# Expert sums, convolution taps and two products of a Mamba and mixture-of-experts block move from VectorE to ScalarE and GpSimd

## The chip, the cores and the metric

The kernel runs on one core of one Trainium2 chip. The core has a TensorE for matrix products, a VectorE, a ScalarE, a GpSimd and a SyncE, which here only issues DMAs. The metric is the device time of one execution in microseconds (us). Each engine works through its own instructions in order; it stands when the next one waits for another engine.

## The reference

Input: x of 4 x 1024 rows of 128 features, fp32. Three parts follow each other, each with a layernorm in front and added to x:

```
x = x + 0.5 * ffn(layernorm(x))
x = x + mamba(layernorm(x))
x = x + 0.5 * ffn(layernorm(x))

ffn(x):                                  # 8 experts, all of them for every row
  cw = softmax(x @ w_router) * softmax((x @ w_gating) / 0.1);  cw = cw / (sum(cw) + 1e-9)
  out = sum over e of cw[:, e] * ((silu(x @ w_gate[e]) * (x @ w_up[e])) @ w_down[e])   # 128 -> 512 -> 128

mamba(x):                                # 256 inner features, 16 states, 4 taps
  xs, z = split(x @ W_in)
  xc = silu(causal_conv4(xs) + conv_b)
  dbl, B, C = split(xc @ W_x);  dt = softplus(dbl @ W_dt + b_dt)
  h[t] = exp(dt * A) * h[t-1] + (dt * xc) * B;   y[t] = sum over states of h[t] * C
  out = ((y + xc * D) * silu(z)) @ W_out
```

## The kernel before

**Tiling.** The 4096 rows are eight blocks of 512 (a batch has two). Tiles have features or hidden units in the 128 partitions and the 512 rows of a block along the free axis. There are 16 feed-forward passes (two per block) and eight Mamba passes. The list `order` gives the sequence of the feed-forward passes: the first part of blocks 0 to 3, then second and first parts by turns, at last second parts alone.

**Clock of the program.** A group is one expert of one pass: four chunks of 128 hidden units. In a group, TensorE first makes gate and up products of four chunks (`gu`, L435 to L437: three matmuls each, since the operands are split into a high and a low fp32r part), then the down products of four chunks of the expert before (`down`, L478, fp32, two instructions each), which add up in the PSUM tile `pd`. There is one `pd` buffer; `pg` and `pu` have two each. A group has eight slots: slots 0 to 3 stand in front of the four `gu`, 4 to 7 in front of the four `down`. All else is hung on slots: pass s starts at slot 64 s, block k of the Mamba part at START[k], and its steps at fixed distances from there (layernorm, transposes, projection `xsproj`, convolution `conv`, `act`, `xproj`, `dtproj`, `softplus`, `dtfin`, then eight pairs of states in `exps`, then `zproj`, `gate`, `outproj`). A pass runs beside a Mamba block most of the time, and TensorE's instructions are in the order of the slots.

**One expert on the other engines.** ScalarE takes SiLU of `pg` into `h` (L438), VectorE multiplies by `pu` (L444), and the down products read `h`. After the fourth down product VectorE multiplies `pd` by the expert's weight, which a DMA has broadcast into `cwb` (L491, for the first expert L488), and GpSimd adds the result to `acc` (L493; in the first and the last pass VectorE does it). When a pass is over, `ffn_end` transposes `acc` on TensorE and adds it to x.

**One state of the Mamba part.** ScalarE makes `da`, exp(dt * A), in two halves (L643). VectorE makes `hb`, `dx` times the broadcast B row (`prod`, L651, written to PSUM), two scans over time (`step`, L656) and the product with C (`read`, L667, back into `da`). GpSimd adds `da` to `y` (L678). The addition is held back until the next `prod` has been issued and waits for its end ("shared SBUF port"). The B and C rows come in `bcb` tiles by DMA, three buffers ahead.

**The planner.** `Plan` keeps a clock per engine with fixed costs and orders VectorE's instructions while the program is written: the product L444 is placed when it should be ready (`now`), small steps go to a list `hi`, the states to a list `lo`. `need` places whatever a next step depends on at once. The order is then fixed; the chip only follows it. `misc` hands out the one PSUM bank that all small products and transposes share, and a new use waits for the last reader.

The convolution before: ScalarE makes the first tap with the bias (L581), VectorE adds the three other taps, two halves each (L587, six instructions per block). `dtfin` multiplies `dt` by `xc` on VectorE (L633), `gate` multiplies the SiLU of z by `y` on VectorE (L702). Table loads on ScalarE stand between SiLU and exponentials.

Of the kernel before, what the change touches and what calls it, by code (L numbers as in the profile page):

```python
# [21 lines left out]
BIG = 10  # L22
START = (80, 168, 272, 368, 472, 568, 672, 784)
N0 = 36
SPR = 1.56
EPI = 130
XP = 23
BU = -4
WIDE = 8
EARLY = 3  # L30
# [9 lines left out]
GT = 4  # L40
PO = 10
FN = -1
FT = 2
# [7 lines left out]
PREL = -12  # L51
FEND = 12
OUT = 3
SL = 0.35
# [73 lines left out]
def tile_macaron_mamba_moe(  # L128
# [78 lines left out]

    wrg = sb.tile([P, P], F32, tag="tmp", bufs=2, name="wrg")
    V.memset(wrg, 0.0)
# [86 lines left out]
    ffn = {}  # L296
    silu_at, h_at = {}, {}

    def ffn_events(s):
# [25 lines left out]
        def logits():  # L325
            plan.need(lambda: "xl" in d)
            xh, xl = d["xh"], d["xl"]
            lt = misc(f"lt_{nm}")
            T.matmul(lt, wrg_h, xh, start=True, stop=False)
            T.matmul(lt, wrg_h, xl, start=False, stop=False)  # L330
            T.matmul(lt, wrg_l, xh, start=False, stop=True)
            ls = d["ls"] = sb.tile([NE2, TB], F32, tag="tmp", bufs=2, name=f"ls_{nm}")
            S.copy(ls, lt[0:NE2, :])
            d["ls_at"] = plan.on_act(0.65, plan.on_pe(0.7, d["low"][4]))
# [50 lines left out]
        def cwt():  # L385
            plan.need(lambda: "cw" in d)
            pt = misc(f"cwt_{nm}")
            for j in range(J):
                T.transpose(pt[0:E, j * P : (j + 1) * P], d["cw"][:, j, :], ident)
            ct = sb.tile([E, TB], F32, tag="tmp", bufs=2, name=f"ct_{nm}")  # L390
            S.copy(ct, pt[0:E, :])
            plan.on_act(0.62, plan.on_pe(0.44, d["cw2"][4]))
            cd = d["cd"] = dr.tile([E, TB], F32, tag="cd", bufs=2, name=f"cd_{nm}")
            nc.sync.dma_start(out=cd, in_=ct)
            for e in range(2):
                load_cw(s, e)
# [18 lines left out]
    def gu(s, c):  # L415
# [29 lines left out]

        h_at[g] = d["h_at", c] = plan.now(mul, 0.6, t, SL)
        if q == 1:
# [13 lines left out]
    def down(s, c):  # L461
        d = ffn[s]
        kind, k = order[s]
        e, f = divmod(c, FC)
        if f == 0:
            plan.need(lambda: not d.get("tmp") or d["tmp"][3])
            d["pd"] = ps.tile([P, TB], F32, tag="pd", bufs=1, name=f"pd_{kind}_{k}_{e}")
            if e + 2 < E:
                load_cw(s, e + 2)
        h = d.pop(("h", c))  # L470
        if len(h) == 2:
            w = d["wds", e][:, :, f * H : (f + 1) * H]
            T.matmul(d["pd"], w[:, 0, :], h[0], start=(f == 0), stop=False)  # L473
            T.matmul(d["pd"], w[:, 0, :], h[1], start=False, stop=False)  # L474
            T.matmul(d["pd"], w[:, 1, :], h[0], start=False, stop=(f == FC - 1))  # L475
            t = plan.on_pe(0.69, d["h_at", c])
        else:
            T.matmul(d["pd"], wd[e][:, f * H : (f + 1) * H], h[0], start=(f == 0), stop=(f == FC - 1))  # L478
            t = plan.on_pe(0.86, d["h_at", c])
        if f < FC - 1:  # L480
            return
        cwb = d.pop(("cwb", e))
        pd = d["pd"]

        def weigh():
            if e == 0:
                d["acc"] = sb.tile([P, TB], F32, tag="acc", bufs=2, name=f"acc_{kind}_{k}")
                V.tensor_tensor(d["acc"], pd, cwb, ALU.mult)  # L488
            else:
                tmp = sb.tile([P, TB], F32, tag="tmp", bufs=2, name=f"tmp_{kind}_{k}_{e}")  # L490
                V.tensor_tensor(tmp, pd, cwb, ALU.mult)  # L491
                eng = V if s in (0, len(order) - 1) else G
                eng.tensor_tensor(d["acc"], d["acc"], tmp, ALU.add)  # L493
                d["acc_at"] = plan.on_pool(1.3, plan.dve)

        d["tmp"] = plan.put(weigh, 0.6, t)

    def ffn_end(s):
        kind, k = order[s]
        d = ffn.pop(s)  # L500
        plan.need(lambda: d["tmp"][3])
        pt = misc(f"fo_{kind}_{k}")
        for j in range(J):
# [10 lines left out]

        plan.reader = plan.put(upd, 0.6, plan.on_pe(0.44, d["acc_at"]))

    carry = {}
    busy = set()
    for k in range(NBLK):
        for q in range(NS // 2):  # L520
            busy.add(START[k] + (WIDE if k else 0) + N0 + 8 * int(SPR * q))

# [11 lines left out]

    riders = []

    def mamba_events(k):
# [38 lines left out]
        def conv(i):  # L576
# [8 lines left out]

            def tap(q):
                V.scalar_tensor_tensor(  # L587
                    cv[:, i, :], xs[:, i, q : q + TB], cw_sb[:, i, q : q + 1], cv[:, i, :],
                    ALU.mult, ALU.add,
                )  # L590
                if q < 3:
                    plan.put(lambda: tap(q + 1), 0.67)
                else:
                    d["conv"] = d.get("conv", 0) + 1
                    d["cv_at"] = plan.dve + 0.1

            plan.put(lambda: tap(1), 0.67, plan.on_act(0.9))

        def act():
            plan.need(lambda: d.get("conv") == ND)  # L600
            xc = d["xc"] = sb.tile([P, ND, TB], F32, tag="xc", bufs=1, name=f"xc_{nm}")
            S.activation(xc, d["cv"], AF.Silu)
            d["xc_at"] = plan.on_act(1.05, d["cv_at"], "silu")

# [26 lines left out]
        def dtfin():  # L631
            dx = d["dx"] = big(f"dx_{nm}")
            plan.put(lambda: V.tensor_tensor(dx, d["dt"], d["xc"], ALU.mult), 1.14, d["spt"])  # L633
            y = d["y"] = sb.tile([P, ND, TB], F32, tag="y", bufs=2, name=f"y_{nm}")
            for i in range(ND):
                S.activation(y[:, i, :], d["xc"][:, i, :], AF.Copy, scale=D_sb[:, i : i + 1])
            plan.on_act(1.22)

        def exps(n):
# [4 lines left out]
            t = plan.on_act(1.22, 0.0, "exp")  # L644
            for f, cost in ((prod, 1.14), (lambda n: step(n, 0), 1.16), (lambda n: step(n, 1), 1.16), (read, 1.14)):
                plan.put(lambda f=f: f(n), cost, t, low=True)

        def prod(n):
            bcb = d["bcb", n]
            hb = d["hb"] = ps.tile([P, ND, TB], F32, tag="hb", bufs=1, name=f"hb_{nm}_{n}")  # L650
            mul = V.tensor_tensor(hb, d["dx"], bcb[:, 0:1, :].to_broadcast([P, ND, TB]), ALU.mult)  # L651
            flush(mul)

# [7 lines left out]
        def read(n):  # L661
# [7 lines left out]
            pump()  # L669
            d["add"] = da  # L670
            if n == NS - 1:
                flush(None)
                d["scanned"] = d["y_at"]

        def flush(after):
            da = d.pop("add", None)
            if da is not None:
                ins = G.tensor_tensor(d["y"], d["y"], da, ALU.add)  # L678
                d["y_at"] = plan.on_pool(2.4, plan.dve)
                if after is not None:  # L680
                    tc.add_manual_dep(
                        ins.ins, after.ins.name, mybir.DependencyInfo(mybir.DependencyClass.Sync, mybir.DependencyReason.DATA),
                        reason="shared SBUF port",
                    )

# [10 lines left out]
        def gate():  # L696
# [3 lines left out]

            def mul():
                V.tensor_tensor(d["yg"], d["yg"], d["y"], ALU.mult)  # L702
                d["gated"] = plan.dve + 0.1

            plan.put(mul, 1.14, d["scanned"])

        def outproj():
            plan.need(lambda: "gated" in d)
            po = misc(f"po_{nm}")
# [11 lines left out]

            plan.reader = plan.put(upd, 0.6, plan.on_pe(1.8, d["gated"]))

        w = WIDE if k else 0

        def free_slot(t):
# [7 lines left out]
            (-1 - 2 * e, ln), (NA - e, nrm), (TA, tr), (XS, inproj), (XS, lambda: xsproj(0)), (XS + 2, lambda: xsproj(1)),  # L734
            (XS + CV, lambda: conv(0)), (XS + CV + 2, lambda: conv(1)), (AP + w, act), (XP + w, xproj),
            (XP + w + 2, lambda: dtproj(0)), (XP + w + 4, lambda: dtproj(1)), (free_slot(28 + w), softplus), (DF + w, dtfin),
        ]
        for q in range(NS // 2):
            t = N0 + 8 * int(SPR * q) + w
# [8 lines left out]
        ev += [  # L748
            (EPI + v, lambda: zproj(0)), (EPI + v + 2, lambda: zproj(1)), (EPI + v + GT, gate), (EPI + v + PO, outproj),
        ]  # L750
# [4 lines left out]
    def add(base, evs):  # L755
        for t, f in evs:
            events.setdefault(max(0, base + t), []).append(f)
# [3 lines left out]
    for s in range(len(order)):  # L761
        add(8 * GPS * s, ffn_events(s))
        kind, k = order[s]
        if kind == 1 and k + 1 < NBLK:
            add(8 * GPS * s, [(8, lambda k=k: load_x(k + 1))])
        add(8 * GPS * (s + 1), [(FEND, lambda s=s: ffn_end(s))])
    for k in range(NBLK):
# [15 lines left out]
    with tc.manual_schedule(engines={ET.PE, ET.Activation, ET.DVE, ET.Pool, ET.SP}):  # L783
        grp = 0
        while events or done < nst:
            for q in range(FC):
# [3 lines left out]
                if c < nst:  # L790
                    gu(c // (GPS * FC), c % (GPS * FC))
            for q in range(FC):
                for f in events.pop(8 * grp + 4 + q, []):
# [41 lines left out]
```

## Time and profile before

| | |
|---|---|
| median of three runs | 1430.25 us (1429.8 to 1431.17) |
| the profiled execution's own time | 1429.55 us |
| its span, first to last instruction | 1427.7 us |
| TensorE busy (modelled ends) | 1315.0 us, 92% |
| VectorE busy | 1252.9 us, 88% |
| ScalarE busy | 815.0 us, 57% |
| GpSimd busy | 491.2 us, 34% |
| TensorE clock granted, mean | 0.978 |

How to read the lines: `PE` is TensorE, `PEld` its weight loads, `DVE` VectorE, `ACT` ScalarE, `POOL` GpSimd, `SP` SyncE. L491 is line 491 of the kernel. A row of a group gives line, engine, operation, output <- input, shapes and count; then busy time in us and the mean of one in ns; then the idle time of the engine just in front of these instructions and what ended it. A row of the waits gives who waited for whom: us in all, times, longest. The digits over the span are busy tenths in 40 equal slices of 35.7 us. A row of a stretch gives its bounds, its length and each engine's busy time in it. Rows with three numbers and slashes give the shortest, median and longest duration in ns.

### The profile page before, as it was taken

To read this page: it belongs to the slowest core of one execution; us is meant where nothing else is said; L and a number is where in the kernel's file an instruction comes from. 1 tells how busy PE (TensorE), PEld (TensorE's weight loads), DVE (VectorE), ACT (ScalarE), POOL (GpSimd) and SP (SyncE) were. 2 spreads that over 40 slices of the span, in tenths; PEclk is the share of its full clock that TensorE was granted. 3 is DMA by queue.
4 is the path that set the end of the run, shared out by engine and by line. 5 is a ranking of instruction groups with operands and counts; after the bars stand their busy time and mean duration, and the time that the engine had idled before them with its cause. 6 is when DMAs were issued, how large, how long until landed. Compare 5 with 4: busy or idle time off the path is not lost. (4 is left out here: it accounts for less than half of the span.)

```text
span 1427.7 us, 14522 instructions
## 1 busy us (share of the span) xinstructions
PE 1315.0 (92%) x4740; PEld 857.2 (60%) x4740; DVE 1252.9 (88%) x1819; ACT 815.0 (57%) x1220; POOL 491.2 (34%) x275
## 2 busy tenths in 40 slices
PE   6999999998998998897999899999999999996897
PEld 4665666565655665564566556655666566664675
DVE  3454699998999998999999999999999989998797
ACT  4444756756666566555676576566667575651321
POOL 1201234344433343344334433353444434432100
PEclk9999999999999999999999999999999999998999
DMA  3411233332322333333332343322433224230010
GB/s 108 136 45 32 76 106 83 88 94 67 84 83 83 105 87 73 70 89 104 73 91 81 74 113 81 104 82 68 102 84 91 75 66 112 80 89 15 8 55 20
DMA packets 71356, 113.47 MB, mean 79 GB/s; under 512 B 6960, under 2 KB 19568, under 8 KB 71280
## 3 DMA queue, kind: packets, MB, share of 16 engines
q1 hardware_dynamic: 71280, 112.54, 29.3%
q8 instruction: 37, 0.61, 0.2%
q14 instruction: 39, 0.32, 0.1%
HBM read 109.64 MB, written 2.88 MB: 79 GB/s over the span
## 5 line engine op out<-in xcount | busy, mean ns | idle before, releaser
L438 ACT ACTIVATE h<-pg 128x512 f32<-128x512 f32 x512 | 302.1, 598 | 420.0 <-PE pg L437 407.7
L678 POOL TENSOR_TENSOR y_m<-y_m,da_m 128x1024 f32<-128x1024 f32 x128 | 307.5, 2402 | 453.3 <-DVE hb_m L651 371.9
L478 PE MATMUL pd<-h,wd 128*128 128x512 f32 x920 | 418.6, 595 | 0.0
L444 DVE TENSOR_TENSOR h<-h,pu 128x512 f32<-128x512 f32 x512 | 339.7, 680 | 83.9 <-PE pu L437 73.7
L478 PEld LDWEIGHTS pd<-h,wd 128*128 128x128 f32 x920 | 172.7, 190 | 174.0 <-issue 166.1
L435 PE MATMUL pg<-xh_f,wh 128*128 128x512 f32 x512 | 258.1, 504 | 18.4 <-ACT h L438 17.6
L435 PE MATMUL pu<-xh_f,wh 128*128 128x512 f32 x512 | 211.3, 413 | 37.6 <-DVE h L444 36.9
L493 POOL TENSOR_TENSOR acc<-acc,tmp 128x512 f32<-128x512 f32 x98 | 141.9, 1448 | 260.3 <-DVE tmp L491 236.4
L437 PE MATMUL pg<-xh_f,wl 128*128 128x512 f32 x512 | 205.1, 401 | 1.0 <-POOL wl L240 1.0
L436 PE MATMUL pg<-xl_f,wh 128*128 128x512 f32 x512 | 204.4, 399 | 0.0
L436 PE MATMUL pu<-xl_f,wh 128*128 128x512 f32 x512 | 204.1, 399 | 0.0
L437 PE MATMUL pu<-xh_f,wl 128*128 128x512 f32 x512 | 203.9, 398 | 0.0
L651 DVE TENSOR_TENSOR hb_m<-dx_m,bcb_m 128x1024 f32<-128x1024 f32 x128 | 165.6, 1293 | 1.3
L656 DVE TENSOR_TENSOR_SCAN hb_m<-da_m,st_sb,hb_m 128x512 f32<-128x512 f32 x128 | 164.1, 1282 | 1.6
L643 ACT ACTIVATE da_m<-dt_m,A_sb 128x512 f32<-128x512 f32 x256 | 163.7, 710 | 0.6
L656 DVE TENSOR_TENSOR_SCAN hb_m<-da_m,hb_m 128x512 f32<-128x512 f32 x128 | 156.4, 1222 | 1.7
L667 DVE TENSOR_TENSOR da_m<-hb_m,bcb_m 128x1024 f32<-128x1024 f32 x128 | 155.6, 1216 | 1.0
L435 PEld LDWEIGHTS pu<-xh_f,wh 128*128 128x128 f32 x512 | 97.8, 191 | 86.7 <-DVE h L444 67.1
L435 PEld LDWEIGHTS pg<-xh_f,wh 128*128 128x128 f32 x512 | 98.3, 192 | 78.1 <-issue 31.5
L436 PEld LDWEIGHTS pg<-xl_f,wh 128*128 128x128 f32 x512 | 98.6, 193 | 41.9 <-issue 27.1
L437 PEld LDWEIGHTS pg<-xh_f,wl 128*128 128x128 f32 x512 | 98.0, 191 | 25.0 <-POOL wl L240 1.4
L437 PEld LDWEIGHTS pu<-xh_f,wl 128*128 128x128 f32 x512 | 97.4, 190 | 22.9
(109 smaller groups left out, 1180.5 us busy)
## 6 DMA issues: line engine op xcount, KB each, us to landing
bcb_m<-bc_m SPq DMA_DIRECT2D x128, 512.0 KB, 4.9
cwb<-cd_f SPq DMA_DIRECT2D x128, 256.0 KB, 4.1
x<-in_L_attn_x_dram SPq DMA_DIRECT2D x8, 256.0 KB, 5.5
wraw<-in_L_ffn_w_gate_dram SPq DMA_DIRECT2D x8, 256.0 KB, 3.1
wraw<-in_L_ffn_w_up_dram SPq DMA_DIRECT2D x8, 256.0 KB, 5.9
wd<-in_L_ffn_w_down_dram SPq DMA_DIRECT2D x8, 256.0 KB, 5.1
out_dram<-x SPq DMA_DIRECT2D x8, 256.0 KB, 6.3
bc_m<-db_m SPq DMA_DIRECT2D x8, 64.0 KB
```

The costliest lines, as they stand in the source:

```text
L435: T.matmul(o, wh[e][:, i, cols], d["xh"], start=True, stop=False)
L436: T.matmul(o, wh[e][:, i, cols], d["xl"], start=False, stop=False)
L437: T.matmul(o, wl[e][:, i, cols], d["xh"], start=False, stop=True)
L438: S.activation(h[:, q, :], pg, AF.Silu)
L444: V.tensor_tensor(h[:, q, :], h[:, q, :], pu, ALU.mult)
L478: T.matmul(d["pd"], wd[e][:, f * H : (f + 1) * H], h[0], start=(f == 0), stop=(f == FC - 1))
L493: eng.tensor_tensor(d["acc"], d["acc"], tmp, ALU.add)
L643: S.activation(da[:, i, :], d["dt"][:, i, :], AF.Exp, scale=A_sb[:, i, n : n + 1])
L651: mul = V.tensor_tensor(hb, d["dx"], bcb[:, 0:1, :].to_broadcast([P, ND, TB]), ALU.mult)
L656: V.tensor_tensor_scan(hb[:, i, :], d["da", n][:, i, :], hb[:, i, :], 0.0 if first else st_sb[:, i, n : n + 1], ALU.mult, ALU.add,)
L667: V.tensor_tensor(da, hb, bcb[:, 1:2, :].to_broadcast([P, ND, TB]), ALU.mult)
L678: ins = G.tensor_tensor(d["y"], d["y"], da, ALU.add)
```

## The change

The diff below is cut to what the prediction speaks of.

- **Expert sums.** In the 14 passes that are neither first nor last, ScalarE copies `pd` from PSUM to SBUF (`take`): for the first expert to `acc`, else to `tmp`. GpSimd then multiplies by `cwb` and, from the second expert on, adds to `acc`. The copy is placed after the second SiLU of the next group (TAKE) or at the latest before `pd` is used again.
- **Batches on GpSimd.** `pool_put` queues a GpSimd instruction; `pool_run` issues all that are queued, when the next `prod` has been issued, and each of them waits for that `prod`. If no state is planned, or a step needs the result (`pool_need`), they are issued at once without that wait. The additions to `y` take this way too.
- **Blocks 1 to 6** (`fast` is false): the convolution's taps are made on ScalarE, one tap of both halves per call, into tiles of their own, and GpSimd adds them up (three additions of 1024 elements). Step-size product and gate are GpSimd's. Their START is 8 slots earlier and WIDE 8 slots more, so that layernorm, projection and taps come one group earlier and `act` and the states stay at their slots. The output projection comes 4 slots later (POW).
- `ffn_end` of passes 1 to 14 but one comes at slot 15 in place of 12; `tmp` has three buffers in place of two; the planner's costs change a little.

```diff
-START = (80, 168, 272, 368, 472, 568, 672, 784)
+TMP = 3
+TAKE = 2
+START = (80, 160, 264, 360, 464, 560, 664, 784)
-WIDE = 8
+WIDE = (0, 16, 16, 16, 16, 16, 16, 8)
+FAST = (0, 7)
+POW = 4
+FENDS = 15
...
     def down(s, c):
         if f == 0:
+            while takes:
+                takes.pop(0)()
...
+        def take():
+            if e == 0:
+                d["acc"] = sb.tile([P, TB], F32, tag="acc", bufs=2, name=f"acc_{kind}_{k}")
+                S.copy(d["acc"], pd)
+                at = plan.on_act(0.58, t)
+                d["sum"] = pool_put(lambda: G.tensor_tensor(d["acc"], d["acc"], cwb, ALU.mult), 1.25, at)
+            else:
+                tmp = sb.tile([P, TB], F32, tag="tmp", bufs=TMP, name=f"tmp_{kind}_{k}_{e}")
+                S.copy(tmp, pd)
+                at = plan.on_act(0.58, t)
+                pool_put(lambda: G.tensor_tensor(tmp, tmp, cwb, ALU.mult), 1.25, at)
+                d["sum"] = pool_put(lambda: G.tensor_tensor(d["acc"], d["acc"], tmp, ALU.add), 1.25, at)
+            d["tmp"][3] = True
+            if e == E - 1:
+                pool_run(None)
+
+        if edge:
+            d["tmp"] = plan.put(weigh, 0.6, t)
+        else:
+            d["tmp"] = [None, 0, 0, False]
+            takes.append(take)
...
+    def pool_put(fn, cost, ready):
+        it = [fn, cost, ready, False, None]
+        pend.append(it)
+        if not plan.lo:
+            pool_run(None)
+        return it
+
+    def pool_run(after):
+        while pend:
+            it = pend.pop(0)
+            ins = it[0]()
+            it[3], it[4] = True, plan.on_pool(it[1], max(it[2], plan.dve))
+            if after is not None:
+                tc.add_manual_dep(
+                    ins.ins, after.ins.name, ..., reason="shared SBUF port",
+                )
+
+    def pool_need(it):
+        if not it[3]:
+            pool_run(None)
+        return it[4]
...
+        def conv_taps(q):
+            xs = d["xs"]
+            a = big(f"tap{q}_{nm}")
+            for i in range(ND):
+                if q == 0:
+                    S.activation(
+                        a[:, i, :], xs[:, i, 0:TB], AF.Identity,
+                        bias=cb_sb[:, i : i + 1], scale=cw_sb[:, i, 0:1],
+                    )
                 else:
+                    S.activation(a[:, i, :], xs[:, i, q : q + TB], AF.Copy, scale=cw_sb[:, i, q : q + 1])
+                t = plan.on_act(0.61)
+            if q == 0:
+                d["cv"] = a
+            else:
+                d["cv_it"] = pool_put(lambda: G.tensor_tensor(d["cv"], d["cv"], a, ALU.add), 2.4, t)
...
-            plan.put(lambda: V.tensor_tensor(dx, d["dt"], d["xc"], ALU.mult), 1.14, d["spt"])
+            d["dx_it"] = plan.put(lambda: V.tensor_tensor(dx, d["dt"], d["xc"], ALU.mult), 1.14, d["spt"]) if fast else pool_put(lambda: G.tensor_tensor(dx, d["dt"], d["xc"], ALU.mult), 2.4, d["spt"])
...
             mul = V.tensor_tensor(hb, d["dx"], bcb[:, 0:1, :].to_broadcast([P, ND, TB]), ALU.mult)
-            flush(mul)
+            pool_run(mul)
...
+            it = pool_put(lambda: G.tensor_tensor(d["y"], d["y"], da, ALU.add), 2.4, plan.dve)
             if n == NS - 1:
-                flush(None)
-                d["scanned"] = d["y_at"]
+                d["scanned"] = it
...
+            d["gated"] = pool_put(lambda: G.tensor_tensor(d["yg"], d["yg"], d["y"], ALU.mult), 2.4, plan.dve)
...
+            ev = [(XS + CV + 2 * q, lambda q=q: conv_taps(q)) for q in range(4)] + ev
...
+                if q == TAKE - 1:
+                    while takes:
+                        takes.pop(0)()
```

More of the change, by code (lines that the diff above doesn't have):

```diff
@@ L206, in tile_macaron_mamba_moe @@
     V.memset(nhalf, -0.5)
-    wrg = sb.tile([P, P], F32, tag="tmp", bufs=2, name="wrg")
+    wrg = sb.tile([P, P], F32, tag="tmp", bufs=TMP, name="wrg")
     V.memset(wrg, 0.0)
@@ L297, in tile_macaron_mamba_moe @@
     silu_at, h_at = {}, {}
+    takes = []
     def ffn_events(s):
@@ L331, in logits @@
             T.matmul(lt, wrg_l, xh, start=False, stop=True)
-            ls = d["ls"] = sb.tile([NE2, TB], F32, tag="tmp", bufs=2, name=f"ls_{nm}")
+            ls = d["ls"] = sb.tile([NE2, TB], F32, tag="tmp", bufs=TMP, name=f"ls_{nm}")
             S.copy(ls, lt[0:NE2, :])
@@ L389, in cwt @@
                 T.transpose(pt[0:E, j * P : (j + 1) * P], d["cw"][:, j, :], ident)
-            ct = sb.tile([E, TB], F32, tag="tmp", bufs=2, name=f"ct_{nm}")
+            ct = sb.tile([E, TB], F32, tag="tmp", bufs=TMP, name=f"ct_{nm}")
             S.copy(ct, pt[0:E, :])
@@ L444, in mul @@
             V.tensor_tensor(h[:, q, :], h[:, q, :], pu, ALU.mult)
-        h_at[g] = d["h_at", c] = plan.now(mul, 0.6, t, SL)
+        h_at[g] = d["h_at", c] = plan.now(mul, 0.62, t, SL)
         if q == 1:
@@ L483, in down @@
         pd = d["pd"]
+        edge = s in (0, len(order) - 1)
         def weigh():
@@ L489, in weigh @@
             else:
-                tmp = sb.tile([P, TB], F32, tag="tmp", bufs=2, name=f"tmp_{kind}_{k}_{e}")
+                tmp = sb.tile([P, TB], F32, tag="tmp", bufs=TMP, name=f"tmp_{kind}_{k}_{e}")
                 V.tensor_tensor(tmp, pd, cwb, ALU.mult)
[L492 to L496, printed above, removed]
+                V.tensor_tensor(d["acc"], d["acc"], tmp, ALU.add)
+                plan.dve += 0.6
+        def take():
[5 more added lines that the diff above has]
+            else:
+                tmp = sb.tile([P, TB], F32, tag="tmp", bufs=TMP, name=f"tmp_{kind}_{k}_{e}")
+                S.copy(tmp, pd)
[10 more added lines that the diff above has]
+            takes.append(take)
     def ffn_end(s):
@@ L500, in ffn_end @@
         d = ffn.pop(s)
+        while takes:
+            takes.pop(0)()
         plan.need(lambda: d["tmp"][3])
+        at = pool_need(d["sum"]) if "sum" in d else d["tmp"][4]
         pt = misc(f"fo_{kind}_{k}")
@@ L513, in upd @@
                 )
-        plan.reader = plan.put(upd, 0.6, plan.on_pe(0.44, d["acc_at"]))
+        plan.reader = plan.put(upd, 0.6, plan.on_pe(0.44, at))
     carry = {}
@@ L520, in tile_macaron_mamba_moe @@
         for q in range(NS // 2):
-            busy.add(START[k] + (WIDE if k else 0) + N0 + 8 * int(SPR * q))
+            busy.add(START[k] + (WIDE[k]) + N0 + 8 * int(SPR * q))
     stored = {}
@@ L535, in tile_macaron_mamba_moe @@
     riders = []
+    pend = []
+    def pool_put(fn, cost, ready):
[11 more added lines that the diff above has]
+                tc.add_manual_dep(
+                    ins.ins, after.ins.name, mybir.DependencyInfo(mybir.DependencyClass.Sync, mybir.DependencyReason.DATA),
+                    reason="shared SBUF port",
+                )
[3 more added lines that the diff above has]
+        return it[4]
     def mamba_events(k):
@@ L584, in conv, with tap @@
             )
[L586 to L592, printed above, removed]
-                else:
-                    d["conv"] = d.get("conv", 0) + 1
-                    d["cv_at"] = plan.dve + 0.1
-            plan.put(lambda: tap(1), 0.67, plan.on_act(0.9))
-        def act():
-            plan.need(lambda: d.get("conv") == ND)
+            t = plan.on_act(0.61)
+            if True:
+                def tap(q):
+                    V.scalar_tensor_tensor(
+                        cv[:, i, :], xs[:, i, q : q + TB], cw_sb[:, i, q : q + 1], cv[:, i, :],
+                        ALU.mult, ALU.add,
+                    )
+                    if q < 3:
+                        d["tap"] = plan.put(lambda: tap(q + 1), 0.67)
+                    else:
+                        d["conv"] = d.get("conv", 0) + 1
+                        d["cv_at"] = plan.dve + 0.1
+                plan.put(lambda: tap(1), 0.67, t)
+        def conv_taps(q):
[6 more added lines that the diff above has]
+                        bias=cb_sb[:, i : i + 1], scale=cw_sb[:, i, 0:1],
+                    )
+                else:
+                    S.activation(a[:, i, :], xs[:, i, q : q + TB], AF.Copy, scale=cw_sb[:, i, q : q + 1])
+                t = plan.on_act(0.61)
+            if q == 0:
+                d["cv"] = a
+            else:
+                d["cv_it"] = pool_put(lambda: G.tensor_tensor(d["cv"], d["cv"], a, ALU.add), 2.4, t)
+        def act():
+            if fast:
+                plan.need(lambda: d.get("conv") == ND)
+                at = d["cv_at"]
+            else:
+                at = pool_need(d["cv_it"])
             xc = d["xc"] = sb.tile([P, ND, TB], F32, tag="xc", bufs=1, name=f"xc_{nm}")
             S.activation(xc, d["cv"], AF.Silu)
-            d["xc_at"] = plan.on_act(1.05, d["cv_at"], "silu")
+            d["xc_at"] = plan.on_act(1.05, at, "silu")
         def xproj():
@@ L644, in exps @@
             t = plan.on_act(1.22, 0.0, "exp")
-            for f, cost in ((prod, 1.14), (lambda n: step(n, 0), 1.16), (lambda n: step(n, 1), 1.16), (read, 1.14)):
+            if n == 0:
+                if fast:
+                    plan.need(lambda: d["dx_it"][3])
+                else:
+                    t = max(t, pool_need(d["dx_it"]))
+            for f, cost in ((prod, 1.2), (lambda n: step(n, 0), 1.2), (lambda n: step(n, 1), 1.2), (read, 1.2)):
                 plan.put(lambda f=f: f(n), cost, t, low=True)
@@ L669, in read @@
             pump()
-            d["add"] = da
+            it = pool_put(lambda: G.tensor_tensor(d["y"], d["y"], da, ALU.add), 2.4, plan.dve)
             if n == NS - 1:
-                flush(None)
-                d["scanned"] = d["y_at"]
[L675 to L684, printed above, removed]
+                d["scanned"] = it
         def zproj(i):
@@ L699, in gate, with mul @@
             plan.need(lambda: "scanned" in d)
[L701 to L705, printed above, removed]
-        def outproj():
-            plan.need(lambda: "gated" in d)
+            if fast:
+                def mul():
+                    V.tensor_tensor(d["yg"], d["yg"], d["y"], ALU.mult)
+                at = pool_need(d["scanned"])
+                d["gated"] = plan.put(mul, 1.14, at)
+                return
+            d["gated"] = pool_put(lambda: G.tensor_tensor(d["yg"], d["yg"], d["y"], ALU.mult), 2.4, plan.dve)
+        def outproj():
+            if fast:
+                plan.need(lambda: d["gated"][3])
+                at = d["gated"][4]
+            else:
+                at = pool_need(d["gated"])
             po = misc(f"po_{nm}")
@@ L720, in upd @@
                 mixed.add(k)
-            plan.reader = plan.put(upd, 0.6, plan.on_pe(1.8, d["gated"]))
-        w = WIDE if k else 0
+            plan.reader = plan.put(upd, 0.6, plan.on_pe(1.8, at))
+        w = WIDE[k]
+        fast = k in FAST
         def free_slot(t):
@@ L734, in mamba_events @@
             (-1 - 2 * e, ln), (NA - e, nrm), (TA, tr), (XS, inproj), (XS, lambda: xsproj(0)), (XS + 2, lambda: xsproj(1)),
-            (XS + CV, lambda: conv(0)), (XS + CV + 2, lambda: conv(1)), (AP + w, act), (XP + w, xproj),
+            (AP + w, act), (XP + w, xproj),
             (XP + w + 2, lambda: dtproj(0)), (XP + w + 4, lambda: dtproj(1)), (free_slot(28 + w), softplus), (DF + w, dtfin),
         ]
+        if fast:
+            ev = [(XS + CV, lambda: conv(0)), (XS + CV + 2, lambda: conv(1))] + ev
+        else:
+            ev = [(XS + CV + 2 * q, lambda q=q: conv_taps(q)) for q in range(4)] + ev
         for q in range(NS // 2):
@@ L748, in mamba_events @@
         ev += [
-            (EPI + v, lambda: zproj(0)), (EPI + v + 2, lambda: zproj(1)), (EPI + v + GT, gate), (EPI + v + PO, outproj),
+            (EPI + v, lambda: zproj(0)), (EPI + v + 2, lambda: zproj(1)), (EPI + v + GT, gate), (EPI + v + PO + (0 if fast else POW), outproj),
         ]
@@ L765, in tile_macaron_mamba_moe @@
             add(8 * GPS * s, [(8, lambda k=k: load_x(k + 1))])
-        add(8 * GPS * (s + 1), [(FEND, lambda s=s: ffn_end(s))])
+        add(8 * GPS * (s + 1), [(FENDS if 0 < s < len(order) - 1 and order[s] != (1, NBLK - 1) else FEND, lambda s=s: ffn_end(s))])
     for k in range(NBLK):
@@ L791, in tile_macaron_mamba_moe @@
                     gu(c // (GPS * FC), c % (GPS * FC))
+                if q == TAKE - 1:
+                    while takes:
+                        takes.pop(0)()
             for q in range(FC):
```

## The prediction

> **What bounds the kernel now.** I read the engine shares first, then the slices of the span:
>
> ```profile
> PE 1315.0 (92%) x4740; PEld 857.2 (60%) x4740; DVE 1252.9 (88%) x1819; ACT 815.0 (57%) x1220; POOL 491.2 (34%) x275
> ...
> PE   6999999998998998897999899999999999996897
> ...
> DVE  3454699998999998999999999999999989998797
> ```
>
> TensorE looks busiest, but its busy time is modelled, so I check it against the time between its starts. VectorE is at 9 tenths from the sixth slice (180 us) on. Second, the timeline:
>
> ```profile
> 600.17 0.39 PE L435 MATMUL pu<-xh_f,wh 128*128 128x512 f32 x1
> 600.40 0.40 PE L436 MATMUL pu<-xl_f,wh 128*128 128x512 f32 x1
> ...
> 603.67 3.60 PE L478 MATMUL pd<-h,wd 128*128 128x512 f32 x8
> 607.10 1.95 PE L712 MATMUL po_m<-w_out_sb,zs_m 128*128 128x128 f32 x16
> ```
>
> Gate and up matmuls start 0.23 us apart; eight down matmuls take 3.43 us (603.67 to the next at 607.10), so 0.43 each. A group (four chunks, one expert) is 24 x 0.2335 + 8 x 0.428 = 9.03 us of TensorE. Third, two stretches:
>
> ```profile
> core 0: us, PE busy (x) PEld busy (x) DVE busy (x) ACT busy (x) POOL busy (x), PEclk, DMA share, GB/s
> 223.10:941.20 718.10, 661.57 (x2344) 420.57 (x2342) 675.47 (x947) 455.13 (x671) 287.48 (x156) 0.98 0.32 86
> 70.70:97.70 27.00, 27.00 (x97) 18.00 (x96) 13.97 (x26) 10.95 (x17) 2.36 (x1) 1.00 0.16 42
> ```
>
> The second row is three groups without the Mamba part: 27.0 us, 9.0 a group, VectorE half idle, so 9.03 is TensorE's own pace. The first row runs from slot 168 to slot 672, five Mamba periods, 63 groups (252 SiLUs at L438). TensorE needs there 63 x 9.03 = 569; five blocks' projections and transposes, 16 x 0.43 + 16 x 0.12 + 0.5 = 9.3 each, 46; and 7.9 passes' transposes and logits at 2.6 (three at 0.23, sixteen small ones at about 0.11), 20. Together **635 us of 718**: 83 us are lost. VectorE is busy 675 of 718. It is the bound; the waits agree:
>
> ```profile
> PE pu L435 <- DVE h L444: 36.9, 48, 2.6
> ACT xn_f L284 <- DVE nb_f L276: 15.5, 2, 8.7
> POOL y_m L678 <- DVE hb_m L651: 371.9, 92, 9.5
> ```
>
> TensorE waits for the product of SiLU and up; ScalarE stands 8.7 us at once for a layernorm's result, with SiLUs queued behind it; GpSimd mostly waits for VectorE.
>
> **The parts and their prices.** Rows:
>
> ```profile
> L491 DVE TENSOR_TENSOR tmp<-pd,cwb 128x512 f32<-128x512 f32 x112 | 76.2, 681 | 36.9 <-PE pd L478 27.4 <-PE pd L475 4.0 <-issue 3.1
> L587 DVE SCALAR_TENSOR_TENSOR cv_m<-xs_m,cw_sb,cv_m 128x512 f32<-128x512 f32 x48 | 39.4, 838 | 0.3
> L633 DVE TENSOR_TENSOR dx_m<-dt_m,xc_m 128x1024 f32<-128x1024 f32 x8 | 12.5, 1563 | 0.0
> L702 DVE TENSOR_TENSOR zs_m<-zs_m,y_m 128x1024 f32<-128x1024 f32 x8 | 10.8, 1350 | 0.4 <-POOL y_m L678 0.4
> L570 ACT COPY xs_m<-xs_m 128x512 f32<-128x512 f32 x16 | 9.4, 588 | 16.5 <-PE xs_m L569 16.5
> L636 ACT ACTIVATE y_m<-xc_m,D_sb 128x512 f32<-128x512 f32 x16 | 10.6, 713 | 0.0
> L678 POOL TENSOR_TENSOR y_m<-y_m,da_m 128x1024 f32<-128x1024 f32 x128 | 307.5, 2402 | 453.3 <-DVE hb_m L651 371.9 <-ACT da_m L643 26.9 <-DVE da_m L667 20.5
> ```
>
> *Off VectorE:* weighings of 14 of the 16 passes, 112 x 0.68 = 76; taps of six blocks, 36 x 0.838 = 30; step-size products 6 x 1.56 = 9; gates 6 x 1.35 = 8. Sum **124 us**. *Onto ScalarE:* 112 PSUM copies at the row of L570, 66; 36 tap activations at the row of L636 (SBUF to SBUF, scale per partition), 26. Sum 92, to about 907. Copy and Identity bring no table load in this trace (none stands at L570 or L581). *Onto GpSimd:* 112 products at 1.29 (the shortest common time of L493's additions), 144; 18 convolution sums, 6 step-size products and 6 gates at 2.40, 72. Sum 216, to about 708 of some 1380.
>
> In the five-period window VectorE loses 63 x 0.68 = 43 and 5 x (5.03 + 1.56 + 1.35) = 40: 675 becomes 593, below TensorE's 635. **The bound passes to TensorE, and the window cannot go below 635.** So what counts is which of the 83 lost us remain, and what is new. I walked TensorE's starts through this window. Before the first `pu` matmul, 27 us (VectorE late); before the first `pg`, 15 (ScalarE, which mostly stood for a layernorm); before the Mamba and router matmuls, 23 (VectorE holds the one `misc` bank or an operand); some 18 are scattered, part of it half-clock after long stalls. After:
> - `pu`: a product may come 1.4 us late before TensorE stands, one scan is 1.28; with VectorE near 88% I keep 8.
> - Mamba and router matmuls: 10; scattered: 7.
> - Layernorms: VectorE is early, but the power at L272 runs on GpSimd, which is now over half busy, and it stands in line behind a batch of 4 to 5 us. Between nothing and 13 x 2.5 us; I keep 8.
> - Taps on ScalarE: four pairs at slots 17, 19, 21, 23 of a block, within one group, 5.8 us beside 2.4 of SiLUs and the copy's 0.6. For blocks 2, 4 and 6 the same group also holds a pair of exponentials with two table loads (2.84 + 2.57), and a layernorm (1.9) or the router's copies. Some 15 us in a group of 9 to 11, less 1.5 of slack: 3 to 5 us. Two such blocks and something for the rest: 10. Without the stretch of down matmuls to hide in, all taps' 26 us would show.
> - The transposes at the end of a pass and the output projection wait for GpSimd chains, given 3 to 4 slots more: 8 x 0.6 = 5.
>
> That is 48, so 683 in place of 718: **35 us** gained. Outside the window: groups 84 to 115 lose 22 us now, of which I take half, 11; block 7's last wait at the output projection (9.6 us) gets 3 shorter; block 0's scans 2; the start and the last pass keep VectorE's path. Together 51: 1429.55 of the profiled execution becomes 1378.5, and against the median, 0.7 higher, **1379**.
>
> DMAs: none is added. The broadcast of the weights for expert e+2 waits for the buffer of e-1, now freed by a GpSimd product instead of VectorE's; it is issued from SP's queue ahead of `bcb` loads, which run three states (some 24 us) ahead of a landing of 4.9. I take nothing; a GpSimd 10 us late would still be covered, at 20 each scan pays the excess.
>
> **Where a rule speaks against it.** First the rows:
>
> ```profile
> L651 DVE TENSOR_TENSOR hb_m<-dx_m,bcb_m x128: 1220/1226/3294, 163.8 to 1290.9; 128x1024 f32<-128x1024 f32 x128
> L493 POOL TENSOR_TENSOR acc<-acc,tmp x98: 1264/1294/2197, 119.0 to 1355.8; 128x512 f32<-128x512 f32 x98
> ```
>
> The product at L651 (two SBUF inputs) takes 1.23 in the median and 3.29 at worst: 2.06 more, nearly one GpSimd addition. The Trainium skill ("SBUF — State Buffer", Who interferes with whom) says why: such an instruction and a GpSimd one that reads SBUF exclude each other, and the later stands until the other is done. The diff ties every batch to the end of such a product. A batch is one `y` addition and 0.8 of a weighing, 2.4 + 0.8 x 2.6 = 4.5 us; the next product comes after two scans and a reading, 3.7 at least, with `h` products between 5 to 7. By the row I take 0.3 us for a third of 80 products, 8 us, inside VectorE's 42 to spare. By the rule, with a whole addition lost each time, 80 x 2.4 = 192, and the kernel would be far slower. The row is nearer, since batches start right behind the product.
>
> Second, the skill ("GPSIMD Engine Reference", 4.1 Engine selection) sends elementwise work to VectorE, GpSimd being about twice as slow with two inputs. The rows agree on the ratio (2.38 against 1.23), and by the rule 216 us replace 124. Here that is no loss as long as GpSimd waits (372 us) for VectorE; it is one if TensorE comes to wait for it.
>
> **Rivals.**
> - *ScalarE becomes the engine that TensorE waits for.* For: in-order, some 76% busy after (455 + 37 + 22 of 680), SiLUs behind copies, taps and table loads. Against: it waits 408 us for `pg` today. If each of 56 pairs of exponentials passes on the copy's 0.6, that is 34: 1413.
> - *TensorE's floor is nearly reached:* half of the 48 stay away in the window and half as much outside: about 1343. Against: single `misc` and `pd` banks.
> - *Slower: the lock at L651.* VectorE is back at today's work when each of the 80 products of the window loses 83 / 80 = 1.04 us. If three batches in four run into the next product (taps make a batch of 12 us) and cost 1.8 each, 1.35 a product, it is 0.31 x 80 = 25 over five periods, some 35 in all: 1465. It decides from 1.04 us a product.
> - *Nothing:* the relief is real in the trace, and TensorE's floor is known; only an exact cancellation gives it.
>
> **Numbers.** Forecast case (1345 to 1395) 0.57; ScalarE's or other waits eat more (1395 to 1427) 0.22; floor 0.08; the lock, slower, 0.11; no change 0.02. Within 0.2%, about what a measurement of this kernel can tell, is 1427.4 to 1433.1. The range 1342 to 1424 leaves out the lock, no change, and 0.06 at the two ends. Faster 0.87.
>
> **What would show it.** Right: VectorE near 1130 us and below 9 tenths in many slices; waits of `pu` for VectorE down to a third; `pd` never waits for a copy; TensorE needing 9.0 to 9.5 in groups without a block's front. Wrong: L651's mean well above 1.5 us, `pg` waiting for ScalarE by 40 us or more, transposes of `acc` or `po` standing for GpSimd.

## The result, and the profile after

The changed kernel takes **1474.18 us** (median; 1470.75 to 1476.31), the kernel before 1430.03 beside it: a ratio of 1.0318, 95% interval 1.0278 to 1.0357. It is 44 us slower where 51 us less were forecast. The span of the profiled execution is 1474.5 us (1476.31 in its own time), the mean granted clock 0.965 (0.978 before).

The first part of the page and its slices, of the changed kernel:

```profile
PE 1332.7 (90%) x4740; PEld 868.5 (59%) x4740; DVE 1196.5 (81%) x1659; ACT 888.0 (60%) x1368; POOL 706.8 (48%) x417
...
PE   6998999997999998998999798979888999996797
...
DVE  4454699888877996899699979985888969997797
```

The work moved as planned: GpSimd is at 706.8 us (708 forecast), ScalarE at 888 (907). VectorE has the 160 instructions less that were planned, but its busy time fell only by 56 us, to 1196.5, where 124 were taken off it. Of the 68 that are missing, some 42 are longer instructions: summed one by one, VectorE's durations fell by 82 us. Most of these 42 is time in which an instruction stood on the shared port: the time above the usual duration of the same form went from 34 to 64 us (the median of each form, instructions over 15% above it), and each of the 65 instructions counted there ends behind the end of a GpSimd instruction, later by no more than its own usual duration and 0.15 us. The other 25 us are no new work: in the profile VectorE's instructions overlap by 75 us in place of 100, and busy time counts an overlap once. And although VectorE is below 9 tenths in many slices now, TensorE is not better served.

Stretches of the changed kernel: the five Mamba periods (groups 21 to 84) and groups 84 to 114 behind them, with the columns of the table shown before:

```profile
228.70:957.20 728.50, 668.68 (x2344) 426.12 (x2342) 629.62 (x849) 501.93 (x764) 428.86 (x244) 0.97 0.31 85
957.20:1302.40 345.20, 314.31 (x1102) 200.80 (x1101) 288.74 (x376) 216.56 (x332) 178.56 (x107) 0.96 0.29 80
```

The same groups took 718.1 and 319.3 us before: 10 and 26 us of the loss, with about 5 each in front and at the end. VectorE is at 86% and 84% there. More than half of the loss is thus behind the window that the prediction worked through, in groups for which it took a gain of 11: `pu` waits for VectorE there for 18.1 us in 10 waits, up to 4.9 each, where it was 7.4 in 12, up to 1.7. The waits of the changed kernel:

```profile
PE pu L441 <- DVE h L450: 58.4, 43, 4.9
PE fo L535 <- POOL acc L515: 19.3, 5, 7.2
PE pg L441 <- ACT h L444: 12.0, 7, 4.9
POOL y_m L754 <- DVE hb_m L735: 110.9, 40, 12.6
```

TensorE waits longer for the SiLU products than before (58.4 us against 36.9), although VectorE has a fifth of its time free; it waits for GpSimd at the ends of passes (`fo`), where it never did; and less for ScalarE's SiLU. The rows of the product that the batches are tied to, and of two router instructions:

```profile
L735 DVE TENSOR_TENSOR hb_m<-dx_m,bcb_m x128: 1220/1232/3416, 167.8 to 1314.3; 128x1024 f32<-128x1024 f32 x128
...
L380 DVE TENSOR_TENSOR cw_f<-ex_f x16: 191/193/2294, 24.8 to 1389.4; 128x32 f32<-128x32 f32 x16
...
L384 DVE TENSOR_SCALAR cs_f<-cs_f x16: 169/170/2072, 25.2 to 1390.9; 128x4 f32<-128x4 f32 x16
```

The product's mean rose from 1.293 to 1.404 us, 14 us in all. The router's instructions work on 4 to 64 numbers per partition and usually last 0.2 us, but up to 2.3 us when they stand on the port. The timeline shows how a batch does it (start, duration, engine, line; rows in between are left out):

```profile
352.66 1.23 DVE L735 TENSOR_TENSOR hb_m<-dx_m,bcb_m 128x1024 f32<-128x1024 f32 x1
354.02 1.27 POOL L514 TENSOR_TENSOR tmp<-tmp,cwb 128x512 f32<-128x512 f32 x1 [5.90 <-ACT ex_f L368]
354.28 1.10 DVE L379 TENSOR_TENSOR ex_f<-ex_f,sm_f 128x64 f32<-128x64 f32 x1
355.38 1.29 POOL L515 TENSOR_TENSOR acc<-acc,tmp 128x512 f32<-128x512 f32 x1
355.42 1.30 DVE L380 TENSOR_TENSOR cw_f<-ex_f 128x32 f32<-128x32 f32 x1
356.63 2.38 POOL L754 TENSOR_TENSOR y_m<-y_m,da_m 128x1024 f32<-128x1024 f32 x1
356.97 2.07 DVE L384 TENSOR_SCALAR cs_f<-cs_f 128x4 f32<-128x4 f32 x1
359.39 2.61 DVE L740 TENSOR_TENSOR_SCAN hb_m<-da_m,st_sb,hb_m 128x512 f32<-128x512 f32 x2
361.91 1.26 DVE L450 TENSOR_TENSOR h<-h,pu 128x512 f32<-128x512 f32 x2
362.63 0.80 PE L441 MATMUL pu<-xh_f,wh 128*128 128x512 f32 x1 [4.10 <-DVE h L450]
```

The batch starts behind the product. Three router instructions each end with one GpSimd instruction (at 355.29 and 355.38, 356.67 and 356.72, 359.01 and 359.04): 4.5 us for 0.6 us of work. The scans and the SiLU products stand behind them in VectorE's fixed order, and TensorE stands 4.1 us.

To compare the runs I use one measure besides the time: the **walk**, the time between the starts of neighbouring matmuls above their own pace (0.2335, 0.428 or 0.115 us), by what the next matmul waited for. Before, it gives 45 us for `pu` on VectorE and 19 for `pg` on ScalarE; after, 65 for `pu`, 20 for `fo` on GpSimd and 13 for `pg`. These three rows make 34 of the 47 us of span. The other large part is the half speed of the clock: gate, up and down matmuls that waited for nothing and ran in its half-speed pieces stand 33.5 us above their pace, 15.7 before. Outside these pieces the same matmuls stand 17, 19 before.

### The profile page after: what moved, and what is told of

It is laid out like the page before. It is cut to its first block, busy times and chain, and to the rows that moved or that the text cites. A ratio compares the mean times of both kernels' runs of the same rounds, so it can differ in the third digit from the quotient of the medians.

```text
span 1474.5 us, 14694 instructions
## 1 busy us (share of the span) xinstructions
PE 1332.7 (90%) x4740; PEld 868.5 (59%) x4740; DVE 1196.5 (81%) x1659; ACT 888.0 (60%) x1368; POOL 706.8 (48%) x417
## 5 line engine op out<-in xcount | busy, mean ns | idle before, releaser
L486 PE MATMUL pd<-h,wd 128*128 128x512 f32 x920 | 427.4, 603 | 0.0
L754 POOL TENSOR_TENSOR y_m<-y_m,da_m 128x1024 f32<-128x1024 f32 x128 | 311.1, 2430 | 124.8 <-DVE hb_m L735 110.9
L514 POOL TENSOR_TENSOR tmp<-tmp,cwb 128x512 f32<-128x512 f32 x98 | 129.0, 1317 | 363.6 <-ACT tmp L512 124.1
L441 PE MATMUL pg<-xh_f,wh 128*128 128x512 f32 x512 | 262.9, 513 | 13.0 <-ACT h L444 12.0
L441 PE MATMUL pu<-xh_f,wh 128*128 128x512 f32 x512 | 213.1, 416 | 58.7 <-DVE h L450 58.4
L735 DVE TENSOR_TENSOR hb_m<-dx_m,bcb_m 128x1024 f32<-128x1024 f32 x128 | 179.7, 1404 | 6.5 <-POOL dx_m L712 4.4
L515 POOL TENSOR_TENSOR acc<-acc,tmp 128x512 f32<-128x512 f32 x98 | 130.5, 1332 | 7.7
```

The costliest lines, as they stand in the source:

```text
L441: T.matmul(o, wh[e][:, i, cols], d["xh"], start=True, stop=False)
L515: d["sum"] = pool_put(lambda: G.tensor_tensor(d["acc"], d["acc"], tmp, ALU.add), 1.25, at)
L754: it = pool_put(lambda: G.tensor_tensor(d["y"], d["y"], da, ALU.add), 2.4, plan.dve)
```

## The experiments

Theory A: VectorE's load was the bound, the relief is worth what was forecast, and new waits ate it. Theory B: TensorE waits because single products are placed or arrive late in a fixed order, so a lighter VectorE brings little. A1 and A2 are two forms of A: the expert sums with their batches, or the parts of the Mamba blocks. The ratios are against the kernel before in the same comparison.

### The relief without its price

```diff
+        elif e < E - 1:                      # middle passes: only the last expert is weighed
+            d["tmp"] = [None, 0, 0, True]
...
+            if 0 < k < 7:                    # no taps 1 to 3; likewise dx = dt, yg = y
+                d["conv"] = d.get("conv", 0) + 1
```

> The kernel before, with VectorE's 124 us left out instead of moved: in the 14 middle passes only the last expert is weighed (experts 0 to 6 add nothing, GpSimd's 98 additions go too), and blocks 1 to 6 have no taps 1 to 3, use dt in place of dt * xc, and y in place of y * silu(z). TensorE and ScalarE do what they did. Theory A (VectorE's load was the bound, the relief is worth what was forecast and new waits ate it): 1385 us or less. Theory B (TensorE waits because single products are placed or arrive late in a fixed order, whatever VectorE's load): 1410 or more, waits of pu for VectorE still above 30 us.

Measured: **1400.81 us**, ratio 0.9812 (0.979 to 0.9833): 26 us, half of the forecast, and nothing was paid for it on any engine. VectorE's busy time fell by 106 us, since the last expert is still weighed. GpSimd lost its 98 additions too, and VectorE's time above the usual fell from 34 to 10 us with them, so part of the 26 may be GpSimd's. First part of its page, and its waits:

```profile
PE 1305.5 (93%) x4740; PEld 854.3 (61%) x4740; DVE 1146.9 (82%) x1673; ACT 814.4 (58%) x1220; POOL 349.3 (25%) x177
```

```profile
PE pu L435 <- DVE h L444: 41.5, 37, 3.5
PE pg L435 <- ACT h L438: 10.0, 8, 3.5
```

With VectorE at 82%, the wait of `pu` is 41.5 us, where it was 36.9 (walk: 47 against 45). VectorE's idle gaps grew from 171 to 249 us: its free time became idle time, not punctual products. What became shorter are the waits for layernorms, router and projections. So both theories are half right: there is a gain from the load, and the largest wait doesn't follow it.

### One part alone

Only the expert sums (all blocks keep the old convolution, step-size product and gate):

```diff
-START = (80, 160, 264, 360, 464, 560, 664, 784)
+START = (80, 168, 272, 368, 472, 568, 672, 784)
-WIDE = (0, 16, 16, 16, 16, 16, 16, 8)
+WIDE = (0, 8, 8, 8, 8, 8, 8, 8)
-FAST = (0, 7)
+FAST = (0, 1, 2, 3, 4, 5, 6, 7)
```

> The changed kernel with all eight blocks on the old way for convolution, step-size product and gate, and the old start slots: only the expert sums go to ScalarE and GpSimd. Theory A1 (GpSimd's batches hold the port against VectorE and the ends of passes wait for them): most of the 44 us loss stays, 1450 or more. Theory A2 (the taps on ScalarE and the long GpSimd batches of the Mamba blocks do it): 1435 or less.

Measured: 1444.24 us, ratio 1.0126 (1.009 to 1.0161). Between the two expectations.

Only the Mamba parts (the sums are weighed on VectorE and added on GpSimd in the batches):

```diff
-            d["tmp"] = [None, 0, 0, False]
-            takes.append(take)
+            d["tmp"] = plan.put(weigh, 0.6, t)      # in all passes
...
+                    d["sum"] = pool_put(lambda: G.tensor_tensor(d["acc"], d["acc"], tmp, ALU.add), 1.25, plan.dve)
```

> The changed kernel with the expert sums weighed on VectorE again and added on GpSimd, in batches: only convolution, step-size product and gate are moved. Theory A1: 1440 or less, and no wait of TensorE for the transposes at the end of a pass. Theory A2: 1450 or more.

Measured: 1434.19 us, ratio 1.005 (1.0035 to 1.0065), with 4 us of `fo` left in the walk. This is nearer to A1, but each part alone loses, 17 us and 7, and together they lose 44: some 20 us come only when GpSimd has both. GpSimd's timeline in the changed kernel, with the longest of the waits at the end of a pass, shows one way:

```profile
829.08 7.28 POOL L672 TENSOR_TENSOR tap_m<-tap_m,tap_m 128x1024 f32<-128x1024 f32 x3
836.32 3.31 POOL L754 TENSOR_TENSOR y_m<-y_m,da_m 128x1024 f32<-128x1024 f32 x1
839.60 1.26 POOL L514 TENSOR_TENSOR tmp<-tmp,cwb 128x512 f32<-128x512 f32 x1
840.94 1.26 POOL L515 TENSOR_TENSOR acc<-acc,tmp 128x512 f32<-128x512 f32 x1
...
842.25 1.12 PE L535 MATMUL fo<-ident,acc 128*128 128x128 f32 x4 [7.18 <-POOL acc L515]
```

The last expert's copy is done at 829.7; its product starts at 839.6, behind the three sums of the convolution and an addition to `y`. The wait of `fo` is 20 us in the walk with both parts, and 7.5 and 3.6 with one.

### The changed kernel without GpSimd's expert sums

```diff
                 S.copy(tmp, pd)
                 at = plan.on_act(0.58, t)
-                pool_put(lambda: G.tensor_tensor(tmp, tmp, cwb, ALU.mult), 1.25, at)
-                d["sum"] = pool_put(lambda: G.tensor_tensor(d["acc"], d["acc"], tmp, ALU.add), 1.25, at)
```

(and likewise the product of expert 0)

> The changed kernel without GpSimd's 112 products and 98 additions of the expert sums: experts 1 to 7 are copied out of PSUM and dropped. ScalarE's copies stay. If GpSimd's part (port and lateness at the ends of passes) is what makes the sums dear: 1435 or less, no wait of the transposes, VectorE's time over the usual near 30. If the copies on ScalarE are: 1455 or more.

Measured: **1409.11 us**, ratio 0.9856 (0.983 to 0.9882), well below the 1435 of the first expectation. The 210 GpSimd instructions of the sums cost **65 us**; all else in the change (the copies on ScalarE, the taps on ScalarE, the Mamba parts on GpSimd) is within some 8 us of the relief without its price. The page and the waits:

```profile
PE 1312.5 (93%) x4740; PEld 860.5 (61%) x4740; DVE 1150.9 (82%) x1659; ACT 887.4 (63%) x1368; POOL 422.3 (30%) x207
```

```profile
PE pu L441 <- DVE h L450: 36.5, 37, 3.1
PE pg L441 <- ACT h L444: 11.6, 8, 3.5
```

The walk loses the 20 us of `fo` and 22 of `pu`; VectorE's time above the usual falls from 64 to 22 us. The time on the clock's half speed, from the trace's clock records, falls from 104 to 61 us (64 before the change). Half of those 43 us, 22, is the most that it can be worth; the matmuls in these pieces show 15 (33.5 to 19 us above their pace). With the other two these make 57 of the 65.

### The ends of the passes

```diff
-FENDS if 0 < s < len(order) - 1 and order[s] != (1, NBLK - 1) else FEND
+FENDS + (0 if s == 9 else 8) if 0 < s < len(order) - 1 and order[s] != (1, NBLK - 1) else FEND
```

> The changed kernel with the transposes at the end of 12 passes one group (8 slots) later. If the 23 us that TensorE stands there for GpSimd are a loss of their own: 1445 to 1455, those waits near zero. If TensorE then stands elsewhere instead, because something else is late by as much: 1465 or more.

Measured: 1460.64 us, ratio 1.024 (1.0218 to 1.0262): 13.5 us less than the changed kernel, between the two expectations. The wait for GpSimd is down from 20 to 4.5 us in the walk; 16 us of waits removed bring 13.5.

### The router's instructions ahead of the batch

```diff
         def prod(n):
+            while router:                    # planned cw1 and cw2
+                it = router.pop(0)
+                if not it[3]:
+                    plan.run(it)
             bcb = d["bcb", n]
```

> The changed kernel with the router's small VectorE instructions, where they are planned but not placed, put ahead of the next product of B and step size instead of behind it, so that they don't meet the GpSimd batch which that product releases. If the lock on them is what makes SiLU products late: VectorE's time over the usual falls from 64 to about 40 us, waits of pu from 65 to about 50, 1455 or less. If not: 1468 or more.

Measured: 1460.58 us, ratio 1.0234 (1.0219 to 1.025): 13.6 less, between the two expectations. The router's instructions on VectorE from L377 to L386 take 34 us in place of 45 (33 before the change), VectorE's time above the usual 53 in place of 64. The size of `pu` was missed: 59 of 65 remain in the walk. The larger part shows at the clock, which went from 0.965 to 0.973: the matmuls in half-speed pieces stand 22.5 us above their pace in place of 33.5. The lock on these few instructions is a cause, and about a third of what the change added to the time above the usual; most of the rest is at the product L735 and in the last passes.

### The planner's slack

`now` fills VectorE until 0.35 us ahead of a product's expected time. A filler of 1.2 to 1.3 us that starts then ends 0.9 us too late. These runs take 0.7:

```diff
-SL = 0.35
+SL = 0.7
```

On the relief without its price:

> The kernel before with the 124 us of VectorE work left out (as in the run with the relief alone) and the planner's slack at 0.7 us in place of 0.35: it starts no filler within 0.7 us of the time at which it expects a SiLU product to be ready. Theory B (TensorE's waits for products come from where the planner puts fillers, not from VectorE's load): waits of pu for VectorE fall from 47 to 30 or less, 1385 or less. Theory A (load): VectorE has the same work, so within 8 us of 1401.

Measured: 1390.34 us, ratio 0.9738 (0.9722 to 0.9755).

```profile
PE pu L435 <- DVE h L444: 24.7, 31, 2.8
```

`pu` falls from 47 to 30 us in the walk (41.5 to 24.7 in the waits), the time by 10.5. The wait follows the placement, as B says, in a kernel whose VectorE has room; 5 us more were expected.

On the changed kernel:

> The changed kernel with the same slack of 0.7. Theory B: waits of pu for VectorE fall from 65 to about 45, 1455 or less. Theory A, or locks alone: 1467 or more.

Measured: 1465.99 us, ratio 1.0271 (1.0255 to 1.0286), between the two expectations. `pu` falls by 29 us, to 36, more than expected, but only 8 us come out: the output projection of block 7 waits 21 us in place of 5 for scans that were put off, and `pg` and the router take 7 and 4 more.

With the two repairs above:

> The changed kernel with the later transposes, the slack of 0.7 and the router's instructions in front. If the three are separate losses they add up: 14 + 15 + 15 less, about 1430. If they are one loss seen at three places: 1450 or more.

Measured: 1438.65 us, ratio 1.0076 (1.0048 to 1.0103). The three add up: 35.5 us, and 13.5, 8.2 and 13.6 one by one. The expectation had counted more for the slack and missed by 9.

With the slack kept at 0.35 in the last four passes:

```diff
+ h_at[g] = d["h_at", c] = plan.now(mul, 0.62, t, 0.7 if s < 12 else SL)
```

> The changed kernel with the later transposes, the router's instructions in front, and the slack of 0.7 in passes 0 to 11: the wait at the output projection of block 7 falls from 21 to about 5, all else as in the run with all three: 1420 to 1430. If the 16 us come back elsewhere: 1435 or more.

Measured: 1432.7 us, ratio 1.0016 (0.9999 to 1.0034). The wait at block 7 is 7 us, but 6 us came out against the run before, not the 14 by which this wait fell. The repairs win back 41 of the 44 us; the change with them is then level with the kernel before.

The kernel before with that slack:

> The kernel before with the slack of 0.7 in passes 0 to 11 (0.35 in the last four, where it held up the last scans of block 7 in the run before). Theory B: waits of pu fall from 45 to about 32, and with VectorE nearly full part of it comes back as scans that are late: 1415 to 1424. If before is bound by VectorE's load, free slots lost to the slack cost as much as they bring: 1426 or more.

Measured: **1490.95 us**, ratio 1.0434 (1.0411 to 1.0456), on the side of the second expectation and 65 us over its bound. Its page and waits:

```profile
PE 1329.7 (89%) x4740; PEld 862.3 (58%) x4740; DVE 1257.1 (84%) x1819; ACT 815.1 (55%) x1220; POOL 495.0 (33%) x275
```

```profile
PE pu L435 <- DVE h L444: 37.5, 43, 3.8
PE lt_f L329 <- DVE xl_f L320: 22.8, 6, 7.9
PE pg L435 <- ACT h L438: 22.8, 8, 10.2
```

`pu` doesn't gain (37.5 against 36.9), and everything that follows scans and layernorms is late. That the fuller VectorE has no places left for its fillers is my reading; no run shows it apart. This is theory A's side: with the larger slack the relief is worth about 100 us (1490.95 - 1390.34), with the old one 26. The two rules differ a little, since the run of 1390.34 has 0.7 in the last four passes too.

The Mamba parts alone with that slack and the router in front:

> The kernel with convolution, step-size product and gate moved but the expert sums on VectorE, with the slack of 0.7 in passes 0 to 11 and the router's instructions in front. By theory B 1434 less about 12 to 15: 1419 to 1423. If the moved Mamba parts are of no use even with a better order: as the kernel before with the same slack, or slower.

Measured: 1478.54 us, ratio 1.0345 (1.0321 to 1.0368). A miss of 56 us, I think for the same reason: with the sums on VectorE the slack takes places that are needed. It is 12 us less than the kernel before with that slack, so the second expectation did not hold either; what of the 12 the moved Mamba parts bring and what the router in front, no run separates.

No run here that computes the whole reference is faster than the kernel before.

## Why the prediction was wrong

- **Bound and loads.** TensorE's pace in a group without waits, the instructions that left VectorE and GpSimd's load came out as written; ScalarE's busy time is 19 us lower. VectorE's busy time, near 1130 us by the prediction's list of signs, is 1196.5. What the floor was used for did not come out: "the bound passes to TensorE" was taken to mean that most of the 83 lost us of the five periods go.
- **The step that failed first: "with VectorE near 88% I keep 8" for `pu`.** In the five periods it is 31 us in the walk (26 before). The relief without its price shows why: at 82% VectorE and with no new work anywhere, `pu` stays. There it moves with the slack (47 to 30): much of it is made by fillers put in front of products. In the full kernel before, the slack did not lower it (37.5 against 36.9). The trace of before hinted at it, no more: of its 14 waits of `pu` of 1 us and over, five come 4 to 9 us after VectorE had last been idle for 0.3 us or more (at 308.7 us a wait of 2.07), so no long backlog had made them; seven have no such idle time in the 12 us before. The relief was worth 26 us, not 51.
- **The step that failed most: the price of the expert sums on GpSimd.** The prediction put the lock "inside VectorE's 42 to spare", so at nothing, and the ends of passes at 5; without the sums the kernel is 65 us faster. The lock was weighed at L651 alone. There it was nearly right: 0.11 us more per product, 14 us in all against 8 for five periods. The router's instructions, which have two SBUF inputs too, or are a `tensor_scalar`, were left out, though the planner likes to place them just behind the product, where the batch starts. Putting the router in front brought 13.6 us. The slower rival named the lock, but at the same product and with 1.04 us each as its threshold; the loss came at a tenth of that. It came near the measured time (1465), but not by its own mechanism. The Trainium skill ("SBUF — State Buffer", Who interferes with whom) has the rule as the timeline shows it, the later one blocked to the end of the other, and it names `tensor_scalar` among those that can contend; the fault was to apply it to one instruction.
- **The ends of passes: "8 x 0.6 = 5".** 15.6 us in the five periods, 20 in all: up to 7.2 at once. The chain of copy, product and addition was costed by its work and not by the queue in front of it, ten us long where a convolution's sums had just been released. Moving the transposes one group later brought 13.5 us.
- **Half-speed clock: "scattered: 7".** Half-speed time went from 64 to 104 us, 13 pieces to 23, and what the matmuls lost in it from 15.7 to 33.5 us. All 13 and all 23 pieces begin within 6 us of the start of a stall of TensorE of 1.6 us or more (11 of 13 in the run without the sums); stalls of 3 us and over went from 6 to 13.
- **Overrated:** ScalarE's taps and the layernorm behind GpSimd, 18 us together. All of `pg`'s wait for ScalarE is 5.2 us there in the walk (15.3 before). The ScalarE rival is out: the copies and taps stay in the run of 1409 us.
- **The signs.** Of those for right, `pd` never waits for a copy, but `pu` waits more and not a third. Of those for wrong, one came: the transposes of `acc` stand for GpSimd.

The cause is settled to this point: without GpSimd's expert sums the kernel is 65 us faster. Two repairs of what GpSimd's batches disturb, the ends and the router, bring 13.5 and 13.6 us by themselves; the slack, which mends the planner's order and brings 10.5 us without any sums too, makes it 41 of 44. How much of the 65 us is the lock and how much GpSimd's queue stays open beyond these two repairs. The clock's part, some 15, isn't a cause of its own here, since its pieces follow the stalls.

## What to carry to other kernels

Taking work off a busy engine need not make it punctual, if its order doesn't let the urgent instruction come first: test with the work left out before paying for it elsewhere. When a batch on GpSimd is tied to the end of a VectorE instruction, look at every instruction that follows there and reads two SBUF operands or is a `tensor_scalar`, the smallest too. A sum that passes through two more queues needs its consumer moved by the length of the queues, not of the work.

## What was not expected of the hardware

A router instruction of 0.17 us (L384, 128 x 4) took 2.07 us beside a GpSimd addition of 2.38; three such instructions each waited for one of three back-to-back GpSimd instructions, so VectorE gets the port between them but loses it again at once. The router's reductions and reciprocals (L377, L378, L383, L385) were never stretched: none of their 64 took more than 0.221 us. And the clock's half speed, in pieces of mostly 3.4 and up to 10.2 us after stalls, was up to 20 us of the loss, (104 - 64) / 2; the matmuls in these pieces show 18.
